# A graph layer with attention and experts: groups of 8, 7, 6, 3 and 1 node tiles instead of 7, 7, 7, 3 and 1, and the work of the first nodes' maxima moved and paused

## The chip, the cores and the metric

One core of one Trainium2 chip. The metric is the device time of one execution in microseconds (us). The core has engines with queues of their own: PE (matrix products), DVE (vector), ACT (activation), POOL (here it issues all indirect DMAs) and SP (here it issues plain DMAs). An engine takes its instructions strictly in the order in which they stand in its queue.

## The reference, cut to what matters

```python
xn = layernorm(x)                                  # x: 3125 nodes x 256
# edges: 100000 pairs (src, dst), sorted by dst
e   = relu((xn[dst] - xn[src]) @ theta_w.T + theta_b + xn[src] @ phi_w.T + phi_b)
gnn = segment_max(e, dst, 3125)                    # 0 for a node without edges
qkv = xn @ w_qkv.T                                 # 8 heads of 64
k, v = instance_norm(k), instance_norm(v)
mix = (q @ (k.T @ v) / 3125 per head) @ w_out.T + b_out
x = x + gnn + mix
t = layernorm(x)
probs = softmax(t @ Wr + br); top 2 of 8 experts, weights made to add up to 1
xt = layernorm(t) * ln_g[e] + ln_b[e]
y_e = gelu(xt @ W1[e] + b1[e]) @ W2[e] + b2[e]     # 256 -> 1024 -> 256
out = x + sum over the 2 chosen experts of weight * y_e
```

The sum over an edge splits: what depends on the destination alone is added after the maximum, so only a row of b = xn @ (phi_w - theta_w).T for each edge's source goes into the maximum.

## The kernel before, in words

**Tiles and groups.** The 3125 nodes are 25 tiles of 128 rows (the last has 53). The edges are put in falling order of their destination, so the last tiles' edges come first. GROUPS names the tiles of five groups, 7, 7, 7, 3 and 1 tiles from the end; STEPS says how many columns of 128 edges each group gets (115, 148, 209, 157 and 98, in all 727). A group's columns are a table of 128 runs: lane p holds STEPS[g] edges that follow each other. The low tiles have the most edges, so small late groups have long stretches of edges.

**Edge stage.** For each column POOL issues one indirect DMA (L125, through `gather`) that fetches 128 rows of b into a slot of a wide buffer of 8 columns; five such buffers go round. DVE folds each column into the one before it (`fold`, L405: a maximum, with a very negative number added where the destination changes), and SP stores each full buffer to `s_d`. This stream of 727 gathers runs from 49 us nearly to the end.

**First nodes.** The 16 nodes with the smallest numbers have so many edges that their last 55 columns are not gathered. `first_nodes` counts early, by one-hot products, which source nodes each of them has; `first_maxima` (L1148 on) takes the maxima later. For each of 7 chunks of 4 tiles it loads rows of b, transposes them (L1180, copied to `bT` at L1183), and for each of the 16 nodes lets PE spread a mask over the lanes (L1193) and lets DVE take a masked maximum (`seen`, L1164, twice for a mask). PACE and PACE_TOKENS say how many steps lie between two masks, without and within a token stage. `bT`, `most`, `ends_of` and the scratch `unread` lie in rows of `xn_hi` that the first two groups have done with.

**Token stage.** When a group's columns are folded, `group` starts: `carry` joins the runs of neighbouring lanes (transposes L413 and L426, scan L418); for every tile POOL fetches the last row of each node's run from `s_d` (`last_rows`), and `token_tile` (L474 on) joins it, adds the rest (L503 to L507), takes the norm's roots, scales, transposes (L540), makes the router's logits (L551) and finds the top two (L554, L555). The roots are a Sqrt on ACT (L522) or, with newton=True, a Newton iteration of small DVE operations (`roots`, L463 to L471). `slots` then ranks the tokens of each half group within their experts, and `dispatch` waits 16 steps and scatters the rows to `xs_d` by indirect DMAs on POOL (L132), two for each tile. CAPS gives 256 places for an expert in the first three groups; what is over goes to the next group's places.

**Experts.** `Stream` runs a group's 8 experts as units on PE (`Units.run`): first layer (L699, 8 steps of 4 matmuls in the record), Gelu on ACT (L701), and in the same steps the second layer of the unit before (L723). Three weight buffers of 2 MB take turns; a load comes in four parts, issued by ACT in the last step of one unit and steps 0, 2 and 5 of the next. Halfway through a unit the next one's rows are transposed (`turn`, L803) and scaled (L814). The fourth group (tiles 1 to 3) isn't scattered: DVE compares places (L784) and PE selects the rows by one-hot products (L793).

**The end.** The last group is tile 0. Its token stage also needs the last 12 columns of each run, picked by `pick_ends` (L1484, after compares L1464 and counts L1470), the carry, and the first nodes' maxima. Then `dense_tile` puts all 128 rows through all 8 experts (L699, L723, scaled by L937, summed by L962 and L964), while `combine` fetches the two results of every other token (L125 with `ys_d` or `ys_last`), weights them (L1506) and stores the output.

**What sets the order.** PE, DVE, ACT and SP run in the order in which the program was written out, and a small planner writes it. Each piece of work is a Python generator; `yield n` puts its next part n steps later, and a step is one indirect DMA on POOL (`tick`, `start`). So a number after `yield` is not a time: it fixes how many folds and other parts stand in front of the next instruction on its engine. PER_TILE (5, 6, 7, 4) is the number of steps between two tiles' token stages; in `token_tile`, `at_once` caps the steps between parts. `clock["tokens"]` is set while a group's token stage is being written out. SEATS = 3 PSUM buffers (`seat`, `leave`) are shared by token stages and masks.

Of the kernel before, what the change touches and what calls it, by code (L numbers as in the profile page):

```python
# [8 lines left out]
F32 = mybir.dt.float32  # L9
BF16 = mybir.dt.bfloat16  # L10
# [9 lines left out]
P = 128  # L20
# [18 lines left out]
NEG = -1.0e38  # L39


GROUPS = ((18, 25), (11, 18), (4, 11), (1, 4), (0, 1))
STEPS = (115, 148, 209, 157, 98)
CAPS = (256, 256, 256, 128)
PARTS = (2, 2, 2, 1)
ROUND = E * CAPS[0]
SPLIT = 11
G = len(GROUPS)
# [3 lines left out]
FIRST = 16  # L52
CHUNK = 4
CHUNKS = -(-NT // CHUNK)
# [4 lines left out]


LAG, STORED, PER_MIX = 6, 9, 5
PER_TILE = (5, 6, 7, 4)
PACE, PACE_TOKENS = 2.2, 4.0
SEATS = 3
TICK = 1.25
ROWS = 256
# [10 lines left out]
def gps_layer(ctx: ExitStack, tc: tile.TileContext, x, src, dst, thetaT, phiT, biases, wq, wkvT,  # L77
              woT, wr, small, w12, b2, out):
    nc = tc.nc
    keep = ctx.enter_context(tc.tile_pool(name="keep", bufs=1))  # L80
# [5 lines left out]
    clock = {"now": 0.0, "edges": 0, "tasks": 0, "pe": 0.0, "seated": 0}  # L86
# [114 lines left out]

    xn_lo = keep.tile([P, SPLIT, D], F32, name="xn_lo")
    xn_hi = keep.tile([P, NT - SPLIT + 1, D], F32, name="xn_hi")
    bT = xn_hi[:, 0:CHUNK, :].rearrange("p i d -> p (i d)").rearrange("p (h n) -> p h n", h=2)
    unread = xn_hi[:, CHUNK, :].bitcast(BF16)
    most = xn_hi[:, CHUNK + 1, 0:2 * FIRST * CHUNKS].rearrange("p (h k c) -> p h k c", h=2, k=FIRST)
    ends_of = xn_hi[:, CHUNK + 2, 0:2 * FIRST].rearrange("p (h k) -> p h k", h=2)

    def xn2(i):
        return xn_lo[:, i, :] if i < SPLIT else xn_hi[:, i - SPLIT, :]  # L210
# [937 lines left out]
    def first_maxima():  # L1148

        nc.vector.memset(most, NEG)  # L1150

        def bank():
            yield from seat()
            at_hand["bank"] = mm.tile([P, 2 * ROWS], F32, name="mm")

        def some(c):
            rows = wide.tile([P, W, D], F32, name="g")
            n = min(CHUNK, NT - c * CHUNK)
            move(nc.sync, rows[:, 0:n, :], b_rows[:, c * CHUNK:c * CHUNK + n, :])
            return rows  # L1160

        def seen(k, c, n, mask_p):
            for h in range(2):
                nc.vector.tensor_tensor_reduce(unread[:, 0:n * P], bT[:, h, 0:n * P], mask_p[:, 0:n * P], 1.0, NEG,  # L1164
                                               op0=OP.add, op1=OP.max, accum_out=most[:, h, k, c:c + 1])
                if h == 1:
                    leave()
                yield 0.5

        of_b = {0: some(0)}  # L1170
        yield 6
        for c in range(CHUNKS):
            i0 = c * CHUNK
            n = min(CHUNK, NT - i0)
            rows = of_b.pop(c)
            for h in range(2):
                yield from bank()
                turned_p = at_hand["bank"]
                for i in range(n):
                    nc.tensor.transpose(turned_p[:, i * P:(i + 1) * P], rows[:, i, h * P:(h + 1) * P], ident)  # L1180
                on_pe(0.28 * n)
                yield 2
                nc.scalar.copy(bT[:, h, 0:n * P], turned_p[:, 0:n * P])  # L1183
                leave()
            held = None
            for k in range(FIRST):
                if k == FIRST - 4 and c + 1 < CHUNKS:
                    of_b[c + 1] = some(c + 1)
                yield from bank()
                mask_p = at_hand["bank"]  # L1190
                for i in range(n):
                    at = k * NT + i0 + i
                    nc.tensor.matmul(mask_p[:, i * P:(i + 1) * P], absent[:, at:at + 1].to_broadcast([P, P]), ident_h,  # L1193
                                     start=True, stop=True)
                on_pe(0.1 * n)
                yield (PACE_TOKENS if "tokens" in clock else PACE) - 1
                if held is not None:
                    yield from seen(k - 1, c, n, held)
                held = mask_p
            yield 1  # L1200
            yield from seen(FIRST - 1, c, n, held)
        nc.vector.tensor_reduce(ends_of, most, AX.X, OP.max)
        yield from bank()
        rows_p = at_hand["bank"][0:FIRST, 0:2 * P].rearrange("k (h p) -> k h p", p=P)
        for h in range(2):
            nc.tensor.transpose(rows_p[:, h, :], ends_of[:, h, :], ident)
        on_pe(0.5)
        yield 4
        nc.vector.tensor_copy(of_first, rows_p.rearrange("k c p -> k (c p)"))
        leave()  # L1210
        clock["firsts"] = True
# [70 lines left out]
    def start(task, at=None):  # L1282
        clock["tasks"] += 1
        tasks.append([clock["now"] if at is None else at, clock["tasks"], task])
# [43 lines left out]
    def dispatch(g, half, i0, i1, top, top_i, taken):  # L1328

        ro = at_hand["route"]  # L1330
        while not all(i in routed for i in range(i0, i1)) or len(taken) < half + (0 < g < G - 2):
            yield 1
        yield 3.2 if g == 0 else 1
        made = []
        at = i0 - GROUPS[g][0]
        rest = shares(ro, i0, i1, top[:, at:at + i1 - i0, :], top_i[:, at:at + i1 - i0, :], made,
                      15 if g == G - 2 and half == 0 else 0)
        start(rest, clock["now"] + next(rest))
        if g == G - 2:
            yield from slots(ro, mm, g, half, i0, i1, made[0], taken, at_hand["ffn"].chosen)  # L1340
            return
        yield from slots(ro, mm, g, half, i0, i1, made[0], taken)
        yield 16
        put = []
        for i in range(i0, i1):
            n = rows_in(i)
            for k in range(2):
                put.append((xs_d[:], slot_i[0:n, k, i:i + 1], xn2(i)[0:n]))
        for one in scatter(*put):
            for of, fetch in asked:  # L1350
                if of < g:
                    apart_in_rows(one, fetch)
            sent.append((g, one))

    def group(g):

        i0, i1 = GROUPS[g]
        start(carry(links, mm, g, clock["last"], chain, carried), clock["now"] + (0.5 if g == G - 1 else 0))
        while "late" not in clock:
            yield 1  # L1360
        clock["tokens"] = g
        ro = at_hand["route"]
        top = ro.tile([P, i1 - i0, E], F32, name="top")
        top_i = ro.tile([P, i1 - i0, E], U32, name="top_i")
        rows = s_d[0:1 + P * COL[g + 1], :]
        slices = range(g + 1)
        if g == G - 2:
            at_hand["ffn"].chosen = ro.tile([P, i1 - i0, E], F32, name="chosen")
        yield STORED if g < G - 1 else 0
        if g == G - 1:  # L1370
            shared = []
            dense = dense_tile(at_hand["act"], at_hand["ffp"], mm, 0, shared, dense_w, next_dense,
                               DENSE, clock, [xn_hi[:, CHUNK + 1 + k, :] for k in range(2)])
            start(routed_tile(0, last_rows(at_hand["tok"], 0, rows), slices, carried, top[:, 0, :], top_i[:, 0, :],
                              newton=True, then=lambda: start(dense), also=ends, at_once=1))
            while 0 not in routed:
                yield 1
            made = []
            yield from shares(ro, 0, 1, top, top_i, made)
            spread(at_hand["act"], 0, made[0])  # L1380
            shared.append(True)
            clock["shared"] = True
            return
        taken = [clock["over"]] if 0 < g < G - 2 else []
        half = (i0 + i1 + 1) // 2
        if g == G - 2:
            half = i1
        waiting = [dispatch(g, k, a, b, top, top_i, taken) for k, (a, b) in enumerate(((i0, half), (half, i1))) if a < b]
        for one in waiting:
            start(one)  # L1390
        for i in range(i0, i1):
            start(routed_tile(i, last_rows(at_hand["tok"], i, rows), slices, carried, top[:, i - i0, :],
                              top_i[:, i - i0, :], newton=0 < g < G - 2, at_once=2 if g == G - 2 else None))
            yield PER_TILE[g]
        while any(t[2] is one for t in tasks for one in waiting):
            yield 1
        clock.pop("tokens")
        if g == 1:
            start(rest_without_edges())
            start(first_maxima())  # L1400
        yield 1 if g == G - 2 else 5
        at_hand["ffn"].add(g)
        at_hand["ffn"].open = g < G - 2
        if g == G - 2:
            start(verdict())
            start(last_ends())
# [202 lines left out]
    with tc.If(wrong > 0), tc.tile_pool(name="general", bufs=1) as ge:  # L1609
# [62 lines left out]
        with tc.tile_pool(name="again", bufs=1) as ag, tc.tile_pool(name="again_w", bufs=2) as aw, \  # L1672
# [15 lines left out]
            for t0 in range(0, T, W):  # L1688
                n = min(W, T - t0)
# [74 lines left out]
```

## Time and profile before

| what | before |
|---|---|
| median of 3 runs | 1182.77 us (1179.74 to 1186.11) |
| the profiled execution | 1182.51 us |
| its span, first to last instruction | 1180.7 us |
| busy PE / DVE / ACT / POOL | 74% / 67% / 28% / 73% |
| mean granted PE clock | 0.868 |
| gathers of b: count, mean, first start, last end | 727, 0.984 us, 48.7 us, 1072.6 us |
| folds (L405): count, mean | 722 recorded, 0.483 us |
| masked maxima (L1164): count, busy | 224, 139.8 us (and 18.2 us to read the accumulators) |
| scatters of the first, second, third group | 379.3 to 405.5, 516.3 to 545.8, 820.0 to 849.8 us |
| row fetches of the third and fourth group | 731.6 to 785.7, 960.0 to 970.2 us |
| first expert matmul of the third group | 859.9 us |
| transposes or selections for the fourth group's first unit | 1005.1 us |
| carry of the last group: scan (L418) | 1085.87 us |
| dense pass: first matmul, end | 1111.8, 1174.3 us |

All of it but the runs' times comes from one profiled execution. A row of groups reads: line, engine, operation, output<-input, count; busy time and mean; idle time of the engine just before them and what ended it. In the records a product of fp32 operands shows as two weight loads and two matmuls. The recorded ends of matmuls are modelled, since PE is a pipeline, so neighbours overlap by some tenths. A busy PE can be at half clock: the clock row says so.

### The profile page before, as it was taken

Reading aid. Unit: us, or ns where it says so; the run is one execution under the profiler, and the core shown is the slowest. Engines: PE = TensorE matmul, PEld = TensorE weight load, DVE = VectorE, ACT = ScalarE, POOL = GpSimd, SP = SyncE. Lnnn points to the kernel's source line nnn. Section 1 sums busy time; section 2 is a strip of 40 time slices with the busy share of each in tenths; the row PEclk is TensorE's granted clock in tenths of the full one; section 3 lists DMA queues with packets and bytes.
Section 4 is the critical chain, followed back from the end, with each engine's and each line's share of the span. In section 5 each row is a group of like instructions: output and inputs, shape, how many; then the busy total and the mean of one; then the engine's idle time right before and its main releaser. Section 6 shows DMA issues by size and latency. Waiting matters only on the chain.

```text
span 1180.7 us, 14516 instructions
## 1 busy us (share of the span) xinstructions
PE 869.3 (74%) x4279; PEld 668.5 (57%) x4279; DVE 791.1 (67%) x2583; ACT 325.9 (28%) x787; POOL 857.1 (73%) x879
## 2 busy tenths in 40 slices
PE   6445888835660098899799898644198989998896
PEld 5323444423330077687478787533177768987796
DVE  7699998864576147943777786889767657534443
ACT  4311233311230043333133232211032325332342
POOL 6677777777777777777777777777777777777361
PEclk9768999968785589899999999955589989999899
DMA  8745677788776369897678997556579987799582
GB/s 274 236 165 191 226 255 254 263 315 299 242 279 213 133 230 314 294 306 297 208 253 306 360 349 287 199 181 218 183 244 330 361 308 238 251 370 356 193 328 88
DMA packets 102663, 306.85 MB, mean 260 GB/s; under 512 B 20515, under 2 KB 44186, under 8 KB 91694
## 3 DMA queue, kind: packets, MB, share of 16 engines
q0 software_dynamic: 42400, 115.28, 30.8%
q1 hardware_dynamic: 29164, 109.58, 24.0%
q10 hardware_dynamic: 31010, 80.97, 19.4%
q8 instruction: 36, 0.59, 0.2%
q14 instruction: 53, 0.43, 0.1%
HBM read 184.99 MB, written 120.75 MB: 259 GB/s over the span
## 4 chain that ended last, share of the span: by engine, by line
PE 29%; DMA 24%; DVE 20%; POOL 15%; issue 9%; ACT 1%; ACTq 0%; POOLq 0%; DVEq 0%; SPq 0%
DMA g<-b_d,srcI 17%; POOL g L125 13%; PE hp L699 7%; PE yp L723 7%; DVE g L405 6%; PE v L1227 3%; DMA r<-s_d,end_i 3%; PE k L1227 2%; POOL xs_d L132 2%; PE bp L280 2%; DVE xn_hi L1164 2%; DMA big<-in_w 2%; PE dots_p L1250 1%; PE mm L498 1%; DMA xs_d<-zero 1%
## 5 line engine op out<-in xcount | busy, mean ns | idle before, releaser
L125 POOL DMA_INDIRECT g<-b_d,srcI x727 | 715.3, 984 | 223.1 <-issue 190.3
L405 DVE SCALAR_TENSOR_TENSOR g<-g,cut 128x256 f32<-128x256 f32 x722 | 349.0, 483 | 238.7 <-DMA g<-b_d,srcI 223.1
L701 ACT ACTIVATE ring<-hp,sm 128x256 f32<-128x256 f32 (+1 forms) x320 | 138.0, 431 | 353.5 <-PE hp L699 350.3
L699 PE MATMUL hp<-xe,big 128*128 128x256 f32 (+1 forms) x768 | 176.9, 355 | 4.4 <-DMA big<-in_w 2.9
L723 PE MATMUL yp<-big,ring 128*128 128x256 f32 x624 | 164.8, 381 | 0.0
L1164 DVE CUSTOM_DVE_ANT_0 xn_hi<-xn_hi,mm 128x512 bf16<-128x512 f32 (+1 forms) x224 | 139.8, 624 | 8.9 <-PE mm L1193 5.7
L699 PEld LDWEIGHTS hp<-xe,big 128*128 128x128 f32 x768 | 131.9, 199 | 21.1 <-ACT ring L701 2.6
L723 PEld LDWEIGHTS yp<-big,ring 128*128 128x128 f32 x624 | 113.1, 192 | 14.3
L699 PE MATMUL hp<-xe,w 128*128 128x256 f32 (+1 forms) x448 | 105.4, 364 | 6.3 <-DMA w<-in_w 3.1
L723 PE MATMUL yp<-w,ring 128*128 128x256 f32 x368 | 103.8, 397 | 0.0
L699 PEld LDWEIGHTS hp<-xe,w 128*128 128x128 f32 x448 | 79.9, 201 | 18.2 <-issue 6.2
L723 PEld LDWEIGHTS yp<-w,ring 128*128 128x128 f32 x368 | 69.7, 201 | 8.8
L1193 PE MATMUL mm<-ident_h,absent 128*128 128x128 bf16 x400 | 44.7, 238 | 40.7 <-DVE xn_hi L1164 33.1
L125 POOL DMA_INDIRECT g<-ys_d,from_i x42 | 41.1, 978 | 33.7 <-DVE g L1506 17.1
L1193 PEld LDWEIGHTS <-absent 128*128 128x128 bf16 x400 | 31.6, 106 | 56.6 <-DVE xn_hi L1164 39.3
L803 PE MATMUL trf<-ident,xn_hi 128*128 128x128 f32 x96 | 15.6, 288 | 54.5 <-DMA xn_hi<-xs_d 54.5
L498 PE MATMUL mm<-cr,oh 128*128 128x257 f32 x118 | 38.8, 466 | 21.8 <-DVE top_i L555 8.2
L814 ACT ACTIVATE xe<-trf,sm 128x256 f32<-128x256 f32 (+1 forms) x64 | 30.8, 535 | 81.8 <-DMA g<-b_d,srcI 49.5
L803 PEld LDWEIGHTS trf<-ident,xn_hi 128*128 128x128 f32 x96 | 12.5, 149 | 57.0 <-DMA xn_hi<-xs_d 54.9
L498 PEld LDWEIGHTS mm<-cr,oh 128*128 128x128 f32 x118 | 25.9, 233 | 28.8 <-issue 12.3
L1236 DVE TENSOR_REDUCE var<-big 128x16 f32<-128x1024 f32 x25 | 30.4, 1216 | 8.7 <-ACT big L1233 8.6
L132 POOL DMA_INDIRECT xs_d<-xn_hi,slot_i x28 | 28.9, 1034 | 8.5 <-issue 7.9
(318 smaller groups left out, 1250.2 us busy)
## 6 DMA issues: line engine op xcount, KB each, us to landing
s_d<-g SPq DMA_DIRECT2D x75, 1024.0 KB, 5.4
big<-in_w ACTq DMA_DIRECT2D x48, 512.0 KB, 8.7
w<-in_w ACTq DMA_DIRECT2D x32, 512.0 KB, 7.0
s_d<-g SPq DMA_DIRECT2D x13, 896.0 KB, 6.0
g<-b_d,srcI POOLq DMA_INDIRECT x727
big<-in_w ACTq DMA_DIRECT2D x4, 2048.0 KB, 10.2
xs_d<-zero ACTq DMA_DIRECT2D x24, 256.0 KB, 2.9
xn_hi<-xs_d ACTq DMA_DIRECT2D x12, 512.0 KB, 3.7
```

The source lines that it names most:

```text
L125: got = nc.gpsimd.indirect_dma_start(out=to, out_offset=None, in_=table, in_offset=row_index(index))
L132: put.append(nc.gpsimd.indirect_dma_start(out=table, out_offset=row_index(index), in_=of, in_offset=None))
L405: nc.vector.scalar_tensor_tensor(g[:, j, :], last, cut[:, t:t + 1], g[:, j, :], op0=OP.add, op1=OP.max)
L498: nc.tensor.matmul(r2, picks[k], carried[g], start=(k == 0), stop=(k == len(slices) - 1))
L699: nc.tensor.matmul(hp[:, 0:n], w1t[:, c, f, :], xe[:, c, 0:n], start=(c == 0), stop=(c == 1))
L701: nc.scalar.activation(hT[f][:, 0:n], hp[:, 0:n], AF.Gelu, bias=sm[:, 4 + f, e:e + 1])
L723: nc.tensor.matmul(yp[r][0:part, :], hT[q][:, r * part:(r + 1) * part], w2t[:, q, :], start=(q == 0), stop=(q == FC - 1 and self.whole))
L814: nc.scalar.activation(xe[:, c, 0:n], self.held["tr", u][:, c, 0:n], AF.Identity, bias=sm[:, 2 + c, e:e + 1], scale=sm[:, c, e:e + 1])
L1164: nc.vector.tensor_tensor_reduce(unread[:, 0:n * P], bT[:, h, 0:n * P], mask_p[:, 0:n * P], 1.0, NEG, op0=OP.add, op1=OP.max, accum_out=mo ...
L1193: nc.tensor.matmul(mask_p[:, i * P:(i + 1) * P], absent[:, at:at + 1].to_broadcast([P, P]), ident_h, start=True, stop=True)
L1227: nc.tensor.matmul(to, xnT(i, c), wkv[:, c, k * INNER:(k + 1) * INNER], start=(c == 0), stop=(c == 1))
L1236: nc.vector.tensor_reduce(var, sq, AX.X, OP.add)
```

## The change

- The groups have 8, 7, 6, 3 and 1 tiles; the columns go with them. The tables are for the same 727 columns in all.
- `first_maxima` starts at the end of the first group's token stage instead of the second's, and stops, before the next mask, for as long as the second or third group's token stage is written out. Its buffers `bT`, `most` and `ends_of` get memory of their own, and `unread` moves to the first tile of the first group.
- The third group takes its roots by Sqrt on ACT, and the steps between its parts are capped at 2, as the fourth group's already were. Its tiles follow each other after 5 steps instead of 7, and its scatters come 10 steps behind `slots` instead of 16.

```diff
-GROUPS = ((18, 25), (11, 18), (4, 11), (1, 4), (0, 1))
-STEPS = (115, 148, 209, 157, 98)
+GROUPS = ((17, 25), (10, 17), (4, 10), (1, 4), (0, 1))
+STEPS = (134, 151, 185, 158, 99)
...
-PER_TILE = (5, 6, 7, 4)
-PACE, PACE_TOKENS = 2.2, 4.0
+PER_TILE = (5, 6, 5, 4)
+BEHIND_SLOTS = (16, 16, 10)
+PACE, PACE_TOKENS, PAUSES = 2.2, 4.0, (1, 2)
...
-    bT = xn_hi[:, 0:CHUNK, :].rearrange("p i d -> p (i d)").rearrange("p (h n) -> p h n", h=2)
-    unread = xn_hi[:, CHUNK, :].bitcast(BF16)
-    most = xn_hi[:, CHUNK + 1, 0:2 * FIRST * CHUNKS].rearrange("p (h k c) -> p h k c", h=2, k=FIRST)
-    ends_of = xn_hi[:, CHUNK + 2, 0:2 * FIRST].rearrange("p (h k) -> p h k", h=2)
+    bT = keep.tile([P, 2, CHUNK * P], F32, name="bT")
+    unread = xn_hi[:, GROUPS[0][0] - SPLIT, :].bitcast(BF16)
+    most = keep.tile([P, 2, FIRST, CHUNKS], F32, name="most")
+    ends_of = keep.tile([P, 2, FIRST], F32, name="ends_of")
...
             for k in range(FIRST):
+                if clock.get("tokens", 0) in PAUSES:
+                    if held is not None:
+                        yield from seen(k - 1, c, n, held)
+                        held = None
+                    while clock.get("tokens", 0) in PAUSES:
+                        yield 1
...
-        yield 16
+        yield BEHIND_SLOTS[g]
...
             start(routed_tile(i, last_rows(at_hand["tok"], i, rows), slices, carried, top[:, i - i0, :],
-                              top_i[:, i - i0, :], newton=0 < g < G - 2, at_once=2 if g == G - 2 else None))
+                              top_i[:, i - i0, :], newton=g == 1, at_once=2 if g > 1 else None))
             yield PER_TILE[g]
...
         clock.pop("tokens")
+        if g == 0:
+            start(first_maxima())
         if g == 1:
             start(rest_without_edges())
-            start(first_maxima())
```

## The prediction, made before the changed kernel ran

> **What bounds the kernel now.** I read the page's 40 slices first (a slice is 29.5 us, a digit tenths of busy).
>
> ```profile
> PE   6445888835660098899799898644198989998896
> DVE  7699998864576147943777786889767657534443
> POOL 6677777777777777777777777777777777777361
> PEclk9768999968785589899999999955589989999899
> ```
>
> POOL is level from start to slice 37: a stream of indirect DMAs. PE has a hole in slices 26 to 29, at half clock, and is nearly full behind it. Next the stretches of time that hole and tail cut out (columns: us, then busy us and instructions of PE, PEld, DVE, ACT, POOL; clock; DMA share; GB/s):
>
> ```profile
> 758.00:856.00 98.00, 35.35 (x152) 25.56 (x151) 80.30 (x321) 9.31 (x21) 74.65 (x77) 0.52 0.56 193
> 856.00:960.00 104.00, 94.21 (x498) 78.10 (x499) 69.84 (x205) 33.56 (x76) 79.19 (x82) 0.96 0.89 314
> 960.00:1005.00 45.00, 40.32 (x194) 33.91 (x194) 32.65 (x146) 21.65 (x40) 34.63 (x35) 0.92 0.75 259
> 1005.00:1112.00 107.00, 95.79 (x599) 87.17 (x599) 50.99 (x165) 33.83 (x96) 67.76 (x70) 0.92 0.78 284
> 1112.00:1175.00 63.00, 58.67 (x387) 52.91 (x385) 24.26 (x59) 23.78 (x65) 31.83 (x33) 1.00 0.68 248
> ```
>
> 758 to 856 is the third group's token stage: PE waits, DVE is busy 80 of 98. From 856 PE works through the third group's eight expert units, then (1005) the fourth's, then (1111.8) the dense pass of tile 0. Third, the costliest groups:
>
> ```profile
> L125 POOL DMA_INDIRECT g<-b_d,srcI x727 | 715.3, 984 | 223.1 <-issue 190.3
> L1164 DVE CUSTOM_DVE_ANT_0 xn_hi<-xn_hi,mm 128x512 bf16<-128x512 f32 (+1 forms) x224 | 139.8, 624 | 8.9 <-PE mm L1193 5.7
> ```
>
> A gather costs 0.98 plus 0.30 of pause; the last one ends at 1072.6, and no full buffer ever holds POOL up before that. Last, the chain that ended last, behind 1040 (start, us, what):
>
> ```profile
> 1041.76 9.96 DMA big<-in_w
> ...
> 1052.36 10.38 DMA big<-in_w
> ...
> 1063.38 11.60 DMA w<-in_w
> ...
> 1083.02 2.59 PE mm L1484 x12
> 1085.83 1.74 PE mm L498 x8
> ...
> 1108.38 3.46 PE yp L723 x16
> ...
> 1170.34 3.90 PE yp L723 x18
> ```
>
> Two limits meet here: the edges (gathers to 1072.6, last fold 1077.6, then tile 0's tokens) and PE, which still owes the fourth group's last two units. The dense inputs lie ready at 1106.4, but PE is free only at 1111.8. So a gain must come out of 1078 to 1112; before the last fold nothing can end the kernel.
>
> **Sizes.** Both builds give POOL the same 842 indirect DMAs (727 gathers, 25 row fetches, 42 scatters, 48 combine fetches) with the last gather at the same place. So 1072.6 stays: cost 0. Counting from the first gather, the last scatter moves from place 274 to 281 in the first group, 383 to 408 in the second, 620 to 592 in the third; the fourth's first row fetch from 706 to 705. At 1.28 to 1.294 us a place: +9, +32, -36 and -1 us. PE has the same expert units as before (three times eight with 256 rows, eight with 128).
>
> Second group, later: its units began at 595 and ended at 758; 32 later is 790. The third's begin not before 820 (below), so 30 us cover it. Third group: the last scatter ended at 850.7, its first unit's transposes began at 855.9; now 814.5 and 820. First expert matmul 4 later: 824.
>
> Third group's units: transposes from 866.9 to 952.3 give 17.1 us a unit, with the maxima's masks between them, as in the new order. Eight: 961, and the last second layer (8 steps of 0.86) 968. Before, units seven and eight took 28 and 25 us, mixed with the fourth group's tokens, and their last second layer lay in the fourth group's first unit. So 36 us earlier in, about 37 earlier out.
>
> What is late next is the fourth group's tokens. Their steps stand on DVE between folds, and a fold waits for its gather. The first expert's compare (L784) ran at 1003.0, behind fold 665; now it stands behind fold 664: 1001.7. PE's turn was 2.1 behind: 1003.8 instead of 1005.1. Of 36 us, 1.3 are left at this point; the rest becomes PE idleness. But the first unit then has no foreign second layer: it took 12.3 us (1007.2 to 1019.5); alone it is 8 steps of 0.58 (two per 1.16, as in the dense pass's first unit) = 4.6.
>
> Here a rule bears. The Trainium skill ("TensorE: Matmul & The Clock Gate", Part 1: The HAM clock gate) says an idle array falls to half clock and needs about 3.4 us of work to return. The row: after the 7.9 us wait at 855.9 twenty matmuls took 7.22, 0.36 each against 0.215: +2.9. The estimate by that page is 3.4/2 = 1.7. I take the row; the difference is 1.2 us. Turn 1.34, scaling 0.7, unit 4.6, clock 2.9: ends 1013.3. The next: 8 x 0.87 + 1.34 = 8.3, then 8.3 plus the end compares (L1470, 2.6): 1021.6 and 1032.5. Before: 1040.8. So about 8 us ahead.
>
> From the fifth unit the weights pace. A load's second part is issued in the first step of the unit before; the chain shows 9.96, 10.38 and 11.60 to its use, units starting at 1051.9, 1062.9 and 1075.1: 11.0 and 12.3 apart. Fifth: issue 1033.4 + 10 = 1043.3; eighth: + 3 x 11.3 = 1077.2. Bounds: with no wait 8.75 each (1069.6), all like the longest 12.3 (1080.2). I take 11.3, since gathers and stores run beside them as in that row. At 1075 PE thus begins not the seventh unit but roughly the eighth.
>
> **Tile 0 and the dense pass.** Behind 1075.1 twelve picks (L1484), five steps and one turn led to the carry at 1085.45, its scan at 1085.87. In the new order the same stand in the eighth unit, without the turn (1.34): 1077.2 + 9.4 = 1086.6; floor 1079 (last fold), top 1089.6. From the scan to the dense inputs: before, xt 9.5, transposes 0.7, copy 0.4, logits 1.0, transposes 0.7, copy 0.4, maximum to picks 1.3, scaling 0.3, less 0.5 that the carry waited for a step: 13.8. Behind the scan PE has three steps and eight second-layer matmuls, 6 us, in gaps. Dense start 1100.4 instead of 1111.8.
>
> It lasted 62.5 us, with a stall of 2.2 at 1153.7: the seventh expert's scaled input stood on DVE behind the 42nd combine operation, which waited for its fetch. Now it stands behind the 36th, but the pass starts 11 earlier against nearly the same fetches: 60.3 to 62.5, I take 61.4. End 1161.8. The combine chain runs beside it: fetches restart at the scan + 23.5 = 1110, 32 x 1.254 + 7.4 of waits = 1158, multiply and store 10: 1168, as late as the dense store, so it adds nothing.
>
> **Maxima.** The same 400 masks and 224 reductions; 42 of them (28.7 + 3.4 us of DVE) leave the third group's token stage and go behind the first group, where DVE was busy 14 of 30 us (413 to 443). Nothing on the path. Their row loads on SP's queue stay seven; both pauses fall before a next load, so no buffer is held through one. Own tiles for bT and maxima take away DVE's 8.9 us wait for a scatter, in idle time: 0.
>
> **Roots, closer steps.** Seven tiles lose 11 small DVE operations (0.16 to 0.2): 13 us, all within the hole. ACT gets a Sqrt (0.20) a tile and table loads: nine in the third stage for none, two in the fourth for six. Here a rule speaks against the change ("ScalarE: Activation LUTs", What ACT_TABLE_LOAD costs): 2.66 us a switch, with a drain of 1.38. The row: 1.28, and in the fourth stage the Sqrt follows its load by 0.02, the next load 0.02 after that; no drain shows. Five more: 6.4 by the row, 13.3 by the rule, on an engine busy 28%; on the stage's path one load, 1.3 or 2.7, less than the room at the scatter. Cost 0.
>
> That room: slot numbers were done at 810.5 and 829.7, their scatters went at 820.0 and 843.3. The wait is now 10 steps for 16. Set against the time at which POOL passed the fold that each stands behind, DVE lagged by 7 to 10 us in the first stage, 16 in the second, 24 in the third (with masks). The new order leaves 20 places of POOL between that fold and the scatter, 25.7 us; with the second stage's 16, nearest because it has expert units and no masks, 9 remain. Beyond it every gather queued behind the scatter on POOL would be late, one for one.
>
> **Sum.** Span 1180.7: scan +0.7, scan to dense start -12.1, dense pass -1.1: 1168.2. The profiled execution took 1182.5, 1.8 more than its span: 1170.0. That execution lies 0.3 below the median of 1182.8.
>
> **Rivals.** (1) As worked out, 1161 to 1174, likeliest 1170: 0.66. (2) The weights eat it: at 12.3 a unit and more DMA time from the fold stream, the eighth starts near 1086, the carry is late too, dense starts near 1109: 1178 (1174 to 1188). For it: DMA share 0.99 at 1033 to 1062. Against: five loads get 57 us where four had 44. 0.21. (3) Slower: POOL stands at the third group's scatter. It decides at a DVE lag over 25.7 us; since 12 us would be won, only 45 us of lag make it slower: 1195. Against: the masks are gone from that stage. 0.05. (4) It does not do what it says, since the second group, 32 later, holds PE to 860, so that the third's 145 us still end at 1005: 1184 (1177 to 1195). It needs 70 us more than the 790 above. 0.03. (5) The load wait is gone altogether: 1158. 0.05.
>
> Of no change this kernel's measurement can tell about 0.5%, 6 us: under 1177 counts as faster. From (1), (5) and a third of (2): 0.77; same 0.16; slower 0.07. The range, 1161 to 1181, ends in (2).
>
> **What would show it.** Right: third group's transposes near 820, last unit out by 970; PE idle before 1002; eighth unit of the fourth group at 1070 to 1080; dense start near 1100; last gather still at 1073. Wrong: POOL pauses over 1 us at the third scatters, units of the fourth group over 13 us apart, or dense inputs waiting on combine operations.

## The result, and the profile after

The changed kernel takes 1175.92 us (median of 22 runs, 1171.48 to 1182.88), the kernel before beside it 1181.97 (22 runs, 1177.50 to 1186.34): ratio 0.9952, 95% interval 0.9937 to 0.9966. It is faster, by 6.05 us where 12.8 were forecast. The profiled execution has a span of 1174.4 us, 6.3 less than before.

The 40 slices of the changed kernel, the same rows as before:

```profile
PE   6445888835672059979899898931998993989996
DVE  7699998863576246787466867784677667542533
POOL 6577777777777777777777777777777777776354
PEclk9868999968785579999999999965999996889899
```

PE's hole, four slices before, is two slices now (763 to 822). A new one stands in the 34th slice (969 to 998), while the last three, which hold the dense pass, look no emptier than before (9, 9, 6 for 8, 9, 6): what is lost there is less than a digit. POOL is as level as before up to the same place.

The stretches cut at the changed kernel's stages (us, then busy us and instructions of PE, PEld, DVE, ACT, POOL; clock; DMA share; GB/s):

```profile
788.00:823.00 35.00, 5.60 (x31) 4.31 (x30) 18.83 (x62) 1.40 (x3) 26.77 (x28) 0.50 0.56 191
823.00:960.00 137.00, 126.55 (x682) 104.11 (x682) 94.26 (x271) 45.65 (x100) 104.40 (x108) 0.98 0.88 313
960.00:1004.00 44.00, 20.92 (x99) 16.27 (x98) 33.55 (x151) 7.93 (x19) 33.34 (x36) 0.73 0.61 208
1004.00:1102.00 98.00, 89.49 (x550) 80.40 (x551) 42.64 (x139) 31.85 (x90) 66.63 (x69) 0.91 0.79 286
1102.00:1168.00 66.00, 61.27 (x388) 55.33 (x387) 30.72 (x79) 23.87 (x65) 30.95 (x32) 0.96 0.73 257
```

The third group's units begin 36 us earlier, and PE then has 23 of 44 us to spare before the fourth group's first unit (960 to 1004). The dense pass begins at 1101.9 instead of 1111.8. But it now takes 66.0 us where it took 62.4.

The chain that ended last, in two stretches of it (start, us, what):

```profile
1044.04 12.43 DMA big<-in_w
...
1068.54 8.80 DMA big<-in_w
...
1084.05 2.59 PE mm L1492 x12
...
1100.21 1.71 PE yp L724 x4
...
1143.80 4.50 issue
1148.30 1.11 PE hp L700 x4
1149.41 0.85 PE yp L724 x2
1150.27 0.85 PE hp L700 x4
1151.12 0.84 PE yp L724 x2
1151.95 0.45 PE hp L700 x4
```

Up to 1101.9 it is the chain that the prediction drew. "issue" at 1143.80 is the news: PE stands for 4.5 us in the middle of the dense pass, and the next four pieces take twice their usual 0.44. In sum the span's 6.3 us are: scan 1.0 later (1086.89 for 1085.87), from scan to dense start 10.9 less (15.0 for 25.9), dense pass 3.6 more.

What PE waited for is on DVE, where the combine pieces run too. A combine piece is up to four tiles: its fetches, two a tile, fill one wide buffer, two DVE operations a tile (L1514) weight what came, and one store on SP takes it out. DVE's own order of time in that stretch (start, us, engine, line, operation, tiles; in brackets the idle time before it and what ended that):

```profile
1137.36 0.48 DVE L1514 SCALAR_TENSOR_TENSOR g<-g,share 128x256 f32<-128x256 f32 x1 [1.63 <-DMA g<-ys_d,from_i]
1143.73 0.48 DVE L1514 SCALAR_TENSOR_TENSOR g<-g,share,x_sb 128x256 f32<-128x256 f32 x1 [5.88 <-DMA g<-ys_d,from_i]
...
1147.46 0.48 DVE L1514 SCALAR_TENSOR_TENSOR g<-g,share 128x256 f32<-128x256 f32 x1 [1.02 <-DMA g<-ys_d,from_i]
1147.86 0.60 DVE L938 TENSOR_SCALAR xe<-xn_hi,sm 128x128 f32<-128x128 f32 x2
```

The last line is the seventh expert's input (L938). It is written at 1147.86, behind the 36th combine operation (L1514), and the 31st of these waited 5.88 us for its fetch. POOL shows why the fetch was late (same columns):

```profile
1127.58 0.95 POOL L126 DMA_INDIRECT g<-ys_d,from_i  x1 [0.30 <-issue]
1138.21 0.94 POOL L126 DMA_INDIRECT g<-ys_d,from_i  x1 [9.69 <-DVE g L1514]
```

The 31st fetch waited 9.69 us for a buffer. The profile puts that down to a DVE operation, but that buffer had held the third combine piece (two of the five wide buffers hold dense weights by then, three go round), whose two operations were done at 1117.6. Left is that piece's store, 53 KB, issued at 1117.63, which must have landed first.

### The profile page after: what moved, and what is told of

The parts are those of the page before. It is cut to its first block, busy times and chain, and to the rows that moved or that the text cites. A ratio compares the mean times of both kernels' runs of the same rounds, so it can differ in the third digit from the quotient of the medians.

```text
span 1174.4 us, 14460 instructions
## 1 busy us (share of the span) xinstructions
PE 860.6 (73%) x4275; PEld 661.1 (56%) x4275; DVE 780.9 (66%) x2511; ACT 333.6 (28%) x800; POOL 853.2 (73%) x879
## 4 chain that ended last, share of the span: by engine, by line
PE 29%; DMA 24%; POOL 18%; DVE 16%; issue 11%; ACT 1%; ACTq 0%; DVEq 0%; POOLq 0%; SPq 0%
DMA g<-b_d,srcI 17%; POOL g L126 15%; PE hp L700 8%; PE yp L724 8%; DVE g L406 4%; DMA r<-s_d,end_i 3%; PE v L1234 3%; POOL xs_d L133 3%; DMA big<-in_w 2%; PE k L1234 2%; PE bp L281 2%; DVE xn_hi L1165 1%; PE dots_p L1257 1%; ACT big L1239 1%; DVE r L504 1%
## 5 line engine op out<-in xcount | busy, mean ns | idle before, releaser
L724 PE MATMUL yp<-big,ring 128*128 128x256 f32 x624 | 170.4, 393 | 0.0
L1165 DVE CUSTOM_DVE_ANT_0 xn_hi<-bT,mm 128x512 bf16<-128x512 f32 (+1 forms) x224 | 140.0, 625 | 11.1 <-PE mm L1200 8.0
L724 PEld LDWEIGHTS yp<-big,ring 128*128 128x128 f32 x624 | 116.2, 198 | 15.0 <-issue 0.6
L724 PE MATMUL yp<-w,ring 128*128 128x256 f32 x368 | 97.8, 379 | 0.0
L1200 PE MATMUL mm<-ident_h,absent 128*128 128x128 bf16 x400 | 41.8, 226 | 44.8 <-DVE most L1165 42.1
L724 PEld LDWEIGHTS yp<-w,ring 128*128 128x128 f32 x368 | 66.2, 191 | 8.0
L804 PE MATMUL trf<-ident,xn_hi 128*128 128x128 f32 x96 | 15.9, 292 | 60.3 <-DMA xn_hi<-xs_d 60.3
L804 PEld LDWEIGHTS trf<-ident,xn_hi 128*128 128x128 f32 x96 | 12.8, 151 | 63.0 <-DMA xn_hi<-xs_d 60.7
L499 PE MATMUL mm<-cr,oh 128*128 128x257 f32 x114 | 30.1, 391 | 15.5 <-issue 10.6
L1234 PE MATMUL v<-wkv,xn_hi 128*128 128x512 f32 x56 | 27.8, 618 | 10.2 <-ACT big L1239 10.2
```

The costliest lines, as they stand in the source:

```text
L499: nc.tensor.matmul(r2, picks[k], carried[g], start=(k == 0), stop=(k == len(slices) - 1))
L724: nc.tensor.matmul(yp[r][0:part, :], hT[q][:, r * part:(r + 1) * part], w2t[:, q, :], start=(q == 0), stop=(q == FC - 1 and self.whole))
L1234: nc.tensor.matmul(to, xnT(i, c), wkv[:, c, k * INNER:(k + 1) * INNER], start=(c == 0), stop=(c == 1))
```

## The experiments

Theory A, first: the scaled input is issued too late on DVE. Theory B: the transfers are too many, and PE would wait for weights or stores instead. For the head of the kernel: theory S, that the third group's gain drowns in PE's slack ahead of the fourth group, and theory D, that it comes back one for one.

**The parts undone.** In p1 the roots go back:

```
-PER_TILE = (5, 6, 5, 4)            +PER_TILE = (5, 6, 7, 4)
-BEHIND_SLOTS = (16, 16, 10)        +BEHIND_SLOTS = (16, 16, 16)
-newton=g == 1, at_once=2 if g > 1  +newton=0 < g < G - 2, at_once=2 if g == G - 2
```

> The changed kernel with one part undone: the third group's roots again by the integer steps on DVE, seven steps between its tiles instead of five and sixteen behind the slot numbers instead of ten. The third group's last scatter stands 21 places of POOL later (613 for 592), so its expert units come 27 us later. Theory S, slack: PE stood idle some 30 us between the third group's last second layer (968) and the fourth group's selection (1002 to 1004), so that the 27 us vanish there: span 1173.5 to 1176, the same as the changed kernel. Theory D, direct: what the third group loses is lost at the end, in part or whole: 1180 to 1195.

In p2 the maxima go back (the third group's tiles seven steps apart, as before):

```
-        if g == 0:
-            start(first_maxima())
         if g == 1:
             start(rest_without_edges())
+            start(first_maxima())
-PAUSES = (1, 2)   +PAUSES = ()      -PER_TILE (5, 6, 5, 4)   +PER_TILE (5, 6, 7, 4)
```

> The changed kernel with one part undone: the first nodes' maxima again start behind the second group and run without pauses, so that their masks lie in the third group's token stage; the third group's tiles are seven steps apart as before, the rest of the change stays. The last scatter stands 11 places later (603 for 592), 14 us, and 42 masks with 32 us of DVE come into the stage. Theory S: the third group's units come 14 to 40 us later and end at 982 to 1008, and only what lies past 1002 costs something: span 1174 to 1180. Theory D: 1188 and more, slower than the kernel before.

In p3 the groups and steps go back to (7, 7, 7, 3, 1) and (115, 148, 209, 157, 98). In this build the row that the masked reductions write and nobody reads is one that the first group's expert inputs are loaded into, so part of these inputs is overwritten; matmuls, transfers and their number are the same.

> The changed kernel with one part undone: groups of 7, 7, 7, 3 and 1 tiles with their steps as before; maxima and roots as changed. The third group's last scatter stands at place 596, only 4 later than with the new groups, with seven tiles' slots and masks in place of six. Theory S: the third group's units begin about 5 us later than in the changed kernel and end far ahead of the fourth group's selection; dense start within 1.5 us of 1102; the tail has the fetches of the kernel before (8, 4, 2, 8, 6, 8, 6, 6), span 1172 to 1176. Theory D: the groups are half of the gain: 1177 to 1180.

In p4 the kernel before gets the new groups and steps, and nothing else.

> The kernel before with the new groups and steps alone; maxima and roots as before. The third group's last scatter stands at place 616 for 620, and the fourth group's first selection at place 769 instead of 764, 6.4 us later, behind fold 704. Theory S: the third group's masks and units still fill PE up to 1002 to 1010 and the fourth group's selection comes 5 us later than before: nothing is won, span 1180 to 1187, ratio 0.999 to 1.005. Theory D: 4 places earlier give 5 us: 1175 to 1176.

Measured, with the two kernels for comparison. The first columns are of the one profiled execution; "stands" is PE's standing time within the dense pass for its inputs, as far as the profile names no other releaser. The ratio is to the kernel before as it ran beside them on the same chip (for p1 to p4 its median was 1182.30), not to the 1181.97 of the first row.

| kernel | third scatters end | dense start | stands | dense end | span | median | ratio, 95% interval |
|---|---|---|---|---|---|---|---|
| before | 850.7 | 1111.8 | 2.2 | 1174.2 | 1180.7 | 1181.97 | |
| changed | 814.8 | 1101.9 | 4.5 | 1167.9 | 1174.4 | 1175.92 | 0.9952 (0.9937 to 0.9966) |
| p1 roots back | 839.4 | 1104.0 | 3.5 | 1167.5 | 1173.9 | 1178.23 | 0.9966 (0.9949 to 0.9984) |
| p2 maxima back | 828.5 | 1100.2 | 8.4 | 1171.0 | 1177.5 | 1175.76 | 0.9937 (0.9909 to 0.9964) |
| p3 old groups | 818.8 | 1095.4 | 6.6 | 1165.4 | 1171.9 | 1172.62 | 0.9909 (0.9881 to 0.9936) |
| p4 groups alone | 844.6 | 1108.8 | 3.5 | 1172.2 | 1178.6 | 1178.68 | 0.9972 (0.9953 to 0.9991) |

Theory S stands for the roots and the maxima: 25 us later scatters (p1) cost 2.1 us at the dense start, 14 us (p2) nothing. p1's own stretch of 960 to 1004 shows where the 25 went:

```profile
960.00:1004.00 44.00, 37.21 (x185) 30.52 (x185) 31.82 (x142) 20.85 (x39) 33.63 (x35) 0.96 0.71 241
```

PE is busy 37 of 44 us there, against 21 in the changed kernel. No single part makes the gain. Undone, neither the maxima nor the roots move the median beyond the overlap of the intervals, and the old groups come out lower (0.9909), not higher: beside the other parts, the new groups are not what the gain needs. Two expectations missed. p3 was to start the dense pass within 1.5 us of 1102 and starts it at 1095.4; p4 was expected at a span of 1180 or more and a ratio of at least 0.999, and has 1178.6 and 0.9972, so the groups alone are worth some 3 us on the kernel before. The table shows something else: the kernels that start the dense pass earliest (p3, p2, changed) stand longest in it. p2 wins 1.7 us at the start and gives back 3.9.

**The tail, first try.** e1 to e4 (inputs two ahead, on the changed kernel and on the one before, the last tile's rows apart, and both) fell on a chip where the kernel before took 1648.48 us (1619 to 1675). Their ratios, 0.9968, 1.0151, 0.9951 and 0.9924 with intervals of 0.010 to 0.022, tell nothing of a stall of 4 us, also where an interval leaves out 1 (e2, e4). Three of them were run again as e5 to e7; what was expected of the one that was not:

> The kernel before, with the same edit alone (scaled inputs two experts ahead). Theory A: its stall of 2.2 us at 1153.7 in the dense pass goes, and nothing else: the dense pass lasts 60.3 instead of 62.5, the span is 1178 to 1179 (1180.7), a ratio of 0.998. Theory B: no change, 1.000, since its pass began 10 us later and its transfers were spread.

**e5: the inputs two experts ahead.**

```
-                held["xe", e] = act.tile([P, 2, ROWS], F32, name="xe")
+                if k % 2 == 0:
+                    held["two"] = act.tile([P, 2, ROWS], F32, name="xe")
+                held["xe", e] = held["two"][:, :, k % 2 * P:(k % 2 + 1) * P]
...
-            between = {1: lambda k=k: scaled(k + 1)}
+            between = {1: lambda k=k: scaled(k + 2)}
```

> The changed kernel, with the dense pass's scaled inputs written two experts ahead instead of one (two experts share one buffer, no memory is added); the earlier try of it fell on a chip where the kernel before took 1648 us. Theory A, the late input: PE's stall of 4.5 us (and 1.7 at half clock behind it) comes from the seventh input standing behind the 36th combine operation on DVE; two ahead it stands behind the 28th, and the dense pass lasts 59.5 to 61 us instead of 65.8. What ends last is then the last combine piece: its last operation at about 1164 and its store, 6.4 later: span 1168.5 to 1171, ratio 0.990 to 0.992. Theory B, the transfers: the DMA engines are full from 1105 to 1140, PE waits for weights or the end for stores: 1173.5 to 1175, ratio 0.995.

Measured: 1177.57 us (12 runs), ratio 0.9969 (0.9950 to 0.9988), no better than the changed kernel. What PE waited for in e5 from 1090 on (engine, line, what for; us in total, times, longest):

```profile
PE yp L724 <- DVE xn_hi L968: 7.0, 3, 5.3
PE mm L541 <- ACT xt L529: 2.3, 1, 2.3
PE hp L700 <- DVE xe L940: 0.6, 1, 0.6
```

Theory A as it was put falls. The input is in time, and PE stands as long (5.3 and 1.2 us) for the accumulate L968, which frees the bank that the next second layer writes, and which stands on DVE behind the same combine operations. Whatever DVE owes PE is late as long as DVE waits for the fetches.

**e6: the fetches earlier.** The third combine piece (the last tile, two fetches) is kept in `bT`, free by then, so that the fourth finds a buffer free:

```
+        if nt == 1:
+            y = bT.rearrange("p h (t d) -> p (h t) d", d=D)
+            rows = [y[:, k * 2:k * 2 + 1, :] for k in range(2)]
+        else:
             y = wide.tile([P, W, D], F32, name="g")
```

> The changed kernel, with the last tile's two fetched rows kept in the tile that held the first nodes' transposed values, so that the fourth combine piece finds a wide buffer free: its eight fetches go at about 1095 to 1105 instead of 1111 to 1121. Theory A: every later fetch is up to 10 us earlier, the seventh input is written before PE needs it at 1143, the stall goes or shrinks to 1, the last fetch is issued near 1150: span 1168 to 1170, ratio 0.989 to 0.992. Theory B: the same bytes have to move behind 1105, weights or stores come later by what the fetches take: 1173.5 to 1175, ratio 0.995.

Measured: 1169.12 us (6 runs), ratio 0.9901 (0.9882 to 0.9920). The profiled execution, with a span of 1163.4, is the fastest of the six, 3.9 us under the median. Its dense pass and tail:

```profile
1097.00:1157.10 60.10, 59.03 (x387) 53.25 (x387) 30.58 (x79) 23.50 (x64) 27.29 (x28) 1.00 0.77 275
1157.10:1163.40 6.30, 0.00 (x0) 0.00 (x0) 0.48 (x1) 0.00 (x0) 0.00 (x0) 0.81 0.10 30
```

PE is busy 59 of 60 us at full clock: no stall. Yet its POOL waits as long, at the same time:

```profile
1125.51 0.95 POOL L126 DMA_INDIRECT g<-ys_d,from_i  x1 [0.30 <-issue]
1137.97 0.94 POOL L126 DMA_INDIRECT g<-ys_d,from_i  x1 [11.52 <-DMA out<-g]
```

Only that this is the 39th fetch and not the 31st, so that the 36 operations ahead of the seventh input have long had theirs. (Here the profile names the store.)

**e7: both edits.**

> Both edits on the changed kernel. Theory A: either of them takes the stall away, together they also take the combine pieces off the end, which is then PE's: dense pass of 59.5 to 61 from 1102, then 6.4: span 1168 to 1169.5, ratio 0.989 to 0.991. Theory B: 1173.5 to 1175.

Measured: 1168.98 us (6 runs), ratio 0.9897 (0.9876 to 0.9918), dense pass 1100.6 to 1161.3: as e6, nothing more.

**e8: the old groups again,** the unread row now in the buffer of the row loads (`unread[c] = rows[:, W - 1, :].bitcast(BF16)`).

> The changed kernel with groups of 7, 7, 7, 3 and 1 tiles and their steps, as in the run of the old groups before it, but with the row that the masks' reductions write and nobody reads put into the buffer of the row loads instead of a row that the first group's expert inputs are loaded into in that build. The last gather stands where it stood. Theory A: the dense pass starts at 1095 to 1103 (1095.4 in the run before), its inputs again wait for combine operations for 4 to 8 us, and the span is 1171 to 1174, ratio 0.990 to 0.994. If instead the shared row had itself moved the time, this run is back at 1176 or above.

Measured: 1172.68 us (6 runs), ratio 0.9928 (0.9907 to 0.9949); dense pass 1097.8 to 1167.5 with stands of 1.4, 1.8 and 3.5. The shared row had not made p3's time.

**f1: e6's edit on the kernel before** (the rows in 2 KB of their own).

> The kernel before, with the last tile's two fetched rows kept in a tile of their own (2 KB a partition that this kernel has free), so that the fourth combine piece finds a wide buffer free, as in the run that did this to the changed kernel. Theory F, the fetch chain: the combine fetches end early or late by their buffers, nearly independent of the change, and what PE loses is how far the dense pass runs ahead of them. The kernel before starts its dense pass 10 us later and lost only the stall of 2.2 us at 1153.7; here it loses none: span 1177.5 to 1179 (1180.7), ratio 0.997 to 0.999; the same edit was worth 6 us on the changed kernel. Theory G: the edit is worth its 6 us by itself, whatever stands before it, because the transfers are spread: 1174 to 1175, ratio 0.994 to 0.995.

Measured: 1178.67 us (12 runs), ratio 0.9979 (0.9957 to 1.0000), span 1178.5: the stall of 2.2 us is gone, and that is all. The same edit takes about 6 us off the changed kernel (0.9901 for 0.9952) and 2 us off the one before: what it takes off is what was lost on the way.

**f2: e6's edit on the old groups** (on e8).

> The changed kernel with the old groups of 7, 7, 7, 3 and 1 tiles (masks' unread row in the row buffer), and with the last tile's fetched rows apart. Theory F: the build of the old groups started its dense pass at about 1098 and lost 6.7 us in three stalls behind combine operations; with the fetches 8 places earlier these go, the pass takes 59.5 to 61, and the span is 1164 to 1167, ratio 0.986 to 0.989, the lowest of all. If the fetch chain is not the cause: 1171 to 1174, as without the edit.

Measured: 1172.18 us (6 runs), ratio 0.9920 (0.9893 to 0.9946): not what was expected. By its median it lies where the expectation put the case that the fetches are not the cause. In the profiled execution the dense pass starts at 1094.7 and stands once, 5.7 us at 1143.5, for the eighth input, which stands on DVE behind combine operations whose fetches got their buffer at 1136.0. So the pass is so early that 36 fetches ahead of that wait are again too few; this reading rests on that one execution.

**f3: fewer transfers.** In the changed kernel, e5, e6, f1 and f2 the long late wait of the fetches ends at 1136.0 to 1138.7, though it stands ahead of different fetches (31, 31, 39, 37, 37). f3 is the changed kernel without the loads of the last three dense experts' weights:

```
-            dense_w[e] = load_w(at_hand["w"][dense_slot[k]], e, nc.scalar)
+            w = at_hand["w"][dense_slot[k]]
+            dense_w[e] = first_of(w[:, 0:HALF]), second_of(w[:, HALF:2 * HALF])
```

> The changed kernel without the three loads of 2 MB that bring the last three dense experts' weights during the dense pass (the units multiply by what lies in those places, so that tile 0's rows come out different); matmuls, stores and fetches stay. In every run so far the wait of the combine fetches ended at 1136 to 1138, at the point where the DMA engines fell from full to half busy. Theory H, the store behind the weights: the 31st fetch waits for a buffer whose store was issued near 1118 and lands only at 1138 because the engines are full of weights; with 6 MB less to move (16 us at 370 GB/s) it goes at 1124 to 1130, PE's stall of 4.5 us goes, the span is 1165 to 1169, ratio 0.987 to 0.992. Theory I, the order alone: the fetches wait for DVE operations and for the order of the stores' queue, whatever the engines carry: the 31st fetch still goes at 1136 to 1139, span 1173 to 1176, ratio 0.994 to 0.997.

Measured: 1167.71 us (6 runs), ratio 0.9883 (0.9858 to 0.9907); dense pass 1100.0 to 1159.3, no stall. POOL's 30th and 31st fetch in it:

```profile
1125.68 1.01 POOL L126 DMA_INDIRECT g<-ys_d,from_i  x1 [0.30 <-issue]
1127.00 0.94 POOL L126 DMA_INDIRECT g<-ys_d,from_i  x1 [0.30 <-issue]
```

The 31st goes at 1127.0 without waiting, 11 us earlier. The stretches behind it, of the changed kernel and then of f3:

```profile
1106.00:1116.00 10.00, 9.98 (x67) 8.47 (x66) 5.20 (x14) 4.24 (x12) 3.89 (x5) 1.00 0.94 350
1116.00:1126.00 10.00, 10.00 (x69) 9.41 (x69) 4.74 (x14) 4.18 (x12) 7.71 (x8) 1.00 0.95 345
1126.00:1136.00 10.00, 10.00 (x70) 9.42 (x70) 4.78 (x11) 4.26 (x12) 2.07 (x2) 1.00 1.02 368
1136.00:1146.00 10.00, 7.76 (x53) 6.95 (x51) 2.69 (x7) 3.30 (x9) 5.96 (x7) 1.00 0.72 273
```

```profile
1116.00:1126.00 10.00, 10.00 (x70) 9.41 (x69) 5.07 (x13) 4.38 (x12) 7.57 (x9) 1.00 0.36 111
1126.00:1136.00 10.00, 10.00 (x71) 9.44 (x71) 5.94 (x14) 4.06 (x12) 7.56 (x9) 1.00 0.65 198
```

DMA share 0.95 and 1.02 against 0.36 and 0.65. What moved in the meantime, by queue (packets, MB, share of the 16 engines; by their sizes and times q10 carries ACT's loads, q0 POOL's fetches, q1 SP's stores). First the changed kernel from 1117.2 to 1122, behind the issue of the 53 KB store, and from 1122 to 1128:

```profile
q10 hardware_dynamic: 75, 1.23, 73.0%
q0 software_dynamic: 117, 0.31, 19.1%
...
q10 hardware_dynamic: 95, 1.29, 56.8%
q0 software_dynamic: 256, 0.70, 36.0%
q1 hardware_dynamic: 40, 0.04, 1.9%
```

Then f3, whose store is issued two microseconds earlier (1115.67), from 1115.8 to 1119.5:

```profile
q0 software_dynamic: 168, 0.44, 37.3%
q1 hardware_dynamic: 54, 0.05, 4.6%
```

In f3 the store's 53 packets of 1 KB are through by 1119.3. In the changed kernel everything ahead of it on SP's own queue has moved by 1117.2, yet none of the store's packets moves before 1122, 42 have moved by 1128.1 and 45 by 1131; the rest go among those of the next store. So theory H is shown: the store that frees the buffer lands late because the DMA engines are full of the dense weights that ACT issues.

Theory B had the right resource and the wrong consequence: the transfers do set when the fetches go on, but the stall can still be taken away, by having more fetches done before that. One sentence of f3's expectation is too wide. The late wait did not end at 1136 to 1138 "in every run so far": in the kernel before it ended at 1143.1, in p2 at 1141.0, in e7 at 1142.5, in p3 at 1130.2. Nor does it end because the load falls: in the changed kernel it ended at 1138.2, the DMA share was still 0.97 from 1138 to 1140, and it fell to 0.47 only from 1142 on. It ends when the store has landed, and the load delays that.

## Why the prediction was right in the head and wrong in the tail

**Sizes and the third group: right.** Scatters ended at 814.8 (814.5), transposes began at 820.05 (820), POOL paused 0.30 at the scatters. The second group did not come in the way.

**What is late next: right in kind, the date in part by luck.** PE stood idle before 1002, and the first expert matmul of the fourth group came at 1004.2. But the selection (L794) was there at 998.6, five us ahead of the 1003.8 forecast. The unit then stood behind the end of the first nodes' maxima: on PE, L1213 waited 2.2 us for their last reduction (L1209), work that the prediction had put at "Nothing on the path". Whether these 2.2 us cost anything at the end is not shown, since PE waits for weights behind them. The half clock weighed there was worth less than either value, 2.9 by the row and 1.7 as estimated by the Trainium skill ("TensorE: Matmul & The Clock Gate", Part 1: The HAM clock gate): the first twenty matmuls took 3.83 us in the chain where 20 at 0.145 (8 in 1.16) are 2.9, so +0.9. The second unit began at 1011.4 where I had 1013.3.

**Weights: right in sum.** The eighth unit was held until 1077.48 (1077.2) by its weights, and the scan came at 1086.9 (1086.6). The fifth unit's 1043.0 (1043.3) is luck: no wait for weights stands ahead of it, and the time went into pieces at half clock from 1029.8 to 1035.3 (0.85 us for 0.44). The waits came at the sixth (1.2 and 3.3 us) and the eighth (0.8). From the sixth to the seventh unit 13.6 us passed, more than the 13 that were named as a sign of rival (2). It did not happen all the same: PE waited 5.3 us in all for fourth-group weights, against 6.0 before.

**Scan to dense start: right in kind.** 10.9 us less for 12.1. Executions of builds with the same head differ by more: e5, e6, e7 and f3 start the pass at 1097.0, 1097.2, 1100.6 and 1100.0.

**Dense pass: here it failed.** The step that failed is the overlap of the dense pass with the combine fetches, and with it the stall in the pass, put at 0 to 2.2 us: "It lasted 62.5 us, with a stall of 2.2 ... Now it stands behind the 36th, but the pass starts 11 earlier against nearly the same fetches: 60.3 to 62.5, I take 61.4", with "The combine chain runs beside it ... so it adds nothing". The pass lasted 66.0. In the kernel before (lines of DVE's, PE's and POOL's order of time):

```profile
1155.42 0.59 DVE L937 TENSOR_SCALAR xe<-xn_hi,sm 128x128 f32<-128x128 f32 x2
...
1155.86 0.70 PE L699 MATMUL hp<-xe,w 128*128 128x128 f32 x4 [2.21 <-issue]
...
1143.05 0.95 POOL L125 DMA_INDIRECT g<-ys_d,from_i  x1 [4.70 <-DMA out<-g]
```

I had seen both sides and not subtracted them: the seventh input was written 7.6 us earlier than before (1147.86 for 1155.42), PE needed it 9.9 earlier (1143.8 for 1153.7). So the stall grew by 2.3, from 2.2 to 4.5. Then PE ran about four pieces at half clock, 3.65 us where they take 1.75: another 1.9, which the stall of 2.2 in the kernel before had not brought. Of these 4.2 the pass shows 3.6; the kernel before stood another 0.35 us for ACT's `ring` ahead of its last unit, which the changed one does not, and the rest was not traced. The combine chain did add nothing at the end (its last operation came at 1163.2, the last matmuls ended at 1167.9); it cost in the middle. I had taken its 7.4 us of waits over from the kernel before, where the long one came ahead of fetch 37; here a wait of 9.69 us came ahead of fetch 31, for a store held up by the dense weights (f3). "Dense inputs waiting on combine operations" was one of the signs of being wrong that I had named. Of the 6.2 us by which the span missed (1174.4 for 1168.2), 4.7 lie in this term (+3.6 for -1.1), 1.2 in the one above and 0.3 in the scan.

That the failed term is what was lost, and not the noise of one execution, rests on the medians: with the fetches out of the way (e6) the changed kernel takes 1169.12, 0.9901 of the kernel before, where 1170.0 was forecast; the kernel before with the same edit (f1) takes 1178.67. The split of the 6.2 us into terms is that of one execution of each kernel.

**Maxima and roots: right about their cost.** The nearest row held for the tables: 14 loads for 9, each 1.283 us, idle ahead of them 0.8 in all for the five at the Sqrt and 0.1 or less for each other line (but 1.8 ahead of the program's first load), so the drain of 1.38 that the Trainium skill adds ("ScalarE: Activation LUTs", What ACT_TABLE_LOAD costs) does not show. Whether the roots are worth 2 us (p1) can't be told from the intervals.

**Open.** Why the old groups' builds (p3, e8, f2) take the scan at 1079 to 1082 and the new groups' at 1083 to 1087 was not tried. It is not the groups alone: the kernel before has the old ones too, and its scan is at 1085.9. How much of the gain each of the other two parts makes is not clear of the noise.

## What to carry to other kernels

When a stage is pulled forward against a chain that stays where it is (here fetches paced by buffers and by full DMA engines), subtract the two dates at every place where the stage needs something from that chain, and also ask what else the same in-order engine owes the stage: curing the one wait that the profile named (e5) only showed the next. If a wait stays when you move what stands behind it (e5), change how much is done before it (e6), or the load on the resource that holds it up (f3). Of all kernels here with the whole computation, the changed one with the last tile's rows apart (e6, e7) is the fastest, about 1169 us against 1176 and 1182.

## What the runs showed of the hardware

A store of 53 KB whose last operand was ready at 1117.6 held its buffer until 1138.2, some 20 us, with the DMA engines 95 to 102% busy, 72% of their time with the loads that ACT had issued; with 6 MB of these loads taken away it had moved by 1119.3.

A stall of PE in the full dense pass cost more than itself only from a certain length on. After the stalls of up to 2.3 us (2.21 in the kernel before, 2.26 and 1.21 in p1, 1.67 and 1.85 in p4, 1.49 in p3, 1.44 and 1.84 in e8, 1.23 in e5) the next pieces took their usual 0.44 us. After those of 2.48 and 2.67 (p3), 3.53 (e8), 4.5 (changed), 5.31 (e5), 5.69 (f2) and 8.36 (p2) PE ran 3.4 to 3.9 us at about half speed, and 6.1 us in e8.

And one chip ran such a program in about 1650 us (in the trace of e2, 1648.5): its gathers took 0.97 us each as elsewhere, but engines stopped for up to 25 us at a time (ACT's Gelu alone waited 239 us for what the profile calls "remote"), with PE busy 58% of the span; the cause was not looked for.
